# The mask gathers of the last four column pairs, moved from layer 0 to the first tiles of layer 1

## The chip, the cores and the metric

The kernel runs on one core of a Trainium2 chip. The metric is the time of one execution on the device in microseconds (us). A profile of one further execution goes with it: times inside the program come from that profile and count from the start of its span.

## The reference, cut to what matters

Four graph layers work on 4096 nodes with 256 features each. The graph is a 4096 x 4096 matrix `adj` of zeros and ones that is sparse and uneven: the first nodes have many neighbours, the late ones few. Every layer computes an attention over the neighbours, adds its input and normalizes.

```
# layer 0: eight heads, a bias from six curvature features
# layer 1: one head
H = X @ W_fc + b_fc
scores = (H @ w_att[:d])[:, None] + (H @ w_att[d:])[None, :] + b_att
alpha  = softmax(where(A > 0, scores, -1e9), axis=1)
x      = layernorm(x + alpha @ H)
# layer 2: four heads, elu, a residual and a second normalization
# layer 3: three attention layers in a row
```

In layer 1 the row's own score falls out of the softmax, so that a neighbour's weight depends on the neighbour alone, and the layer is a product of the mask (0 or 1) with prepared rows, divided by a sum.

## The kernel before, in words

**Pairs and lists.** Layers 1 to 3 work on `NP` = 16 "pairs" of `PW` = 256 output rows. A pair is either dense (all 32 tiles of 128 source nodes) or listed: layer 0 builds for it a list of those source nodes that have an edge into the pair, packed into `PAIR_TILES[q]` tiles of 128 nodes. The lists of pairs 1 to 15 have 251 tiles in all; the last four pairs, 12 to 15, have 14, 14, 13 and 13, together 54. In layer 1 the first six pairs are dense (`DENSE`), and the first `LEAD[1]` = 80 tiles that it works on are all dense; after them listed tiles and the remaining dense tiles alternate.

**What layer 0 prepares for the lists.** `list_pair(q)` computes two tables for each list: `pair_idx`, the node numbers, and `cell`, the place of each node's mask row in `adj` transposed. With it, `listed_mask` (L1000) makes one mask tile: POOL issues an indirect DMA that gathers 128 rows of 256 int32 from `adjT` into `pair_m` (L1003, 128 KB), DVE converts them to bytes in `pair_mb` (L1007), and SP writes these to `listed_d` in device memory (L1008). It returns the conversion as a function of its own, so that it can be run later. `job` starts one mask tile for each step of `lane` and runs a conversion when more than three are under way.

**Layer 0 itself.** `rows_by_edges` goes over blocks of up to ten tiles of edges. For each tile POOL gathers 128 rows from `table0` into `g` (L648). For each block DVE takes `d` from `g` (L655), PE and ACT make the pair terms (L657 to L667), DVE multiplies `g` by its weights (L679), and PE adds the rows up into `acc` (L692), beside products that place the edges (L628). Three buffers hold `g`, so the gathers of a block wait until L692 is done with the block three before it. Now and then `Ends0` finishes four chunks of rows: it normalizes them and projects them for layer 1 (L196 to L216). The mask tiles, the list building (L976, L982) and the rows of the one dense chunk (L498 to L525) run between the blocks.

**Layer 1.** `layer1` first prepares 32 tiles of rows: SP loads `V` (L1365), DVE and ACT scale it and split it into two pieces `Vp` (L1359, L1360, L1368), and POOL writes eight parts of `table` (L1370). Then `attend` runs through the sequence of tiles. For each tile `weights` turns a mask tile into `w` (L1382; ACT takes the tiles with odd count, DVE the others), for listed tiles gathers the node rows (L1284, POOL, 16 buffers) and splits them; `products` (L1393) multiplies two tiles behind. `ends_of` finishes a pair: sums, normalization, and the projection for layer 2. SP loads four mask tiles at once (L1278), into six buffers.

**What sets the order.** Each engine works off its own queue in order. Inside `attend`, the orders of PE, DVE and ACT are those of the program text (`manual_schedule`); elsewhere, and for POOL and SP, a scheduler places the instructions when the program is built. POOL has one queue for all gathers and for its table writes.

Of the kernel before, what the change touches and what calls it, by code (L numbers as in the profile page):

```python
# [52 lines left out]
U8 = mybir.dt.uint8  # L53
U16 = mybir.dt.uint16
I32 = mybir.dt.int32
# [6 lines left out]
P = 128  # L62
# [9 lines left out]
PW = 256  # L72
PAIR_TILES = [32, 25, 22, 20, 19, 18, 17, 16, 16, 15, 15, 14, 14, 14, 13, 13]
DENSE = {1: 6, 2: 1, 3: 3}
LEAD = {1: 80, 2: 32, 3: 44}


@with_exitstack
def gnn_stack(ctx: ExitStack, tc: tile.TileContext, a: dict, out: bass.AP):
# [19 lines left out]
    NP = N // PW  # L99
# [4 lines left out]
    keep = ctx.enter_context(tc.tile_pool(name="keep", bufs=1))  # L104
# [3 lines left out]
    def tags(pool, names):  # L108

        count = [0]  # L110

        def ps(shape, name):
            count[0] += 1
            return pool.tile(shape, F32, name=name, tag=names[count[0] % len(names)])
        return ps

    def drain(steps):
        for _ in steps:
            pass
# [201 lines left out]
    def row_tile(k):  # L321
        return epi.tile([P, C], F32, name=f"y{k % 4}", bufs=1)
# [271 lines left out]
    def rows_by_edges(prepared, pair_w, neg_bound, ends, ps, lane, first):  # L594
# [8 lines left out]
        with ExitStack() as st:  # L603
# [149 lines left out]
            ends.until(NC)  # L753
            drain(ends.steps)

    def layer0(proj):
        lin = 1.0 - 0.2
        with ExitStack() as st:
# [60 lines left out]
            lists = st.enter_context(tc.tile_pool(name="l0_list", bufs=2))  # L819
            pool = st.enter_context(tc.tile_pool(name="l0_ps", bufs=1, space=PSUM))  # L820
            ps = tags(pool, ["pa", "pb"])
            lists_ps = st.enter_context(tc.tile_pool(name="l0_list_ps", bufs=1, space=PSUM))

            jobs, dense_jobs = [], []
# [134 lines left out]
            def list_pair(q):  # L959


                A, Q, b = PAIR_TILES[q], NT // 4, q % BP
                at = ats[q // BP]
                cell = lists.tile([P, A], I32, name="cell", bufs=NP - 1)
                rhs = lists.tile([P, NT, 2, A], BF16, name="rhs", bufs=1)
                nc.vector.tensor_tensor(rhs[:, :, 1, :], count.unsqueeze(1)[:, :, 0:A].to_broadcast([P, NT, A]),
                                        at[:, 0, b, :].unsqueeze(2).to_broadcast([P, NT, A]), ALU.is_equal)
                yield
                nc.vector.tensor_tensor(rhs[:, :, 0, :], rhs[:, :, 1, :], tiles.unsqueeze(2).to_broadcast([P, NT, A]), ALU.mult)
                nc.vector.tensor_scalar_mul(rhs[:, :, 1, :], rhs[:, :, 1, :], row)  # L970
                yield
                pl = lists_ps.tile([P, 2, A], F32, name="list_p")

                def products(k, here):
                    for T in range(k * Q, (k + 1) * Q):
                        nc.tensor.matmul(pl, here[:, T - k * Q, :], rhs[:, T], start=T == 0, stop=T == NT - 1)  # L976

                due = []
                for k in range(4):
                    T = slice(k * Q, (k + 1) * Q)  # L980
                    here = lists.tile([P, Q, P], BF16, name="here", bufs=2)
                    nc.vector.tensor_tensor(here, count.unsqueeze(1).to_broadcast([P, Q, P]),  # L982
                                            at[:, 1, b, T].unsqueeze(2).to_broadcast([P, Q, P]), ALU.is_equal)
                    due.append((k, here))
                    yield
                    if len(due) > 1:
                        products(*due.pop(0))
                products(*due.pop(0))
                yield
                x = lists.tile([P, 2, A], F32, name="list")  # L990
                nc.vector.tensor_copy(x, pl)

                nc.vector.scalar_tensor_tensor(x[:, 0], x[:, 0], float(P), x[:, 1], ALU.mult, ALU.add)
                nc.vector.tensor_scalar_add(pair_idx[:, pair_at[q]:pair_at[q] + A], x[:, 0], float(N))
                nc.vector.tensor_scalar(x[:, 1], x[:, 0], float(N), float(N - 1), ALU.add, ALU.min)
                nc.vector.tensor_scalar(cell, x[:, 1], float(N // PW), float(q), ALU.mult, ALU.add)
                jobs.extend([lambda i=i: listed_mask(q, i, cell) for i in range(A)])
                yield

            def listed_mask(q, k, cell):  # L1000

                m = at_pool.tile([P, PW], I32, name="pair_m", bufs=5)
                nc.gpsimd.indirect_dma_start(m[:, :], None, pair_cells, bass.IndirectOffsetOnAxis(ap=cell[:, k:k + 1], axis=0))  # L1003

                def convert():
                    mb = at_pool.tile([P, PW], U8, name="pair_mb")
                    nc.vector.tensor_scalar(mb, m, 0.0, None, ALU.is_gt)  # L1007
                    nc.sync.dma_start(listed_d[:, pair_at[q] + k, :], mb)  # L1008
                return convert
# [150 lines left out]
            at_pool = st.enter_context(tc.tile_pool(name="l0_at", bufs=3))  # L1160

            for ic in range(-(-DENSE[1] * PW // IC)):
                dense_jobs.extend(mask_bytes(at_pool, ic))
            begun, dense_begun = [], []
            lanes = [[edge_lists, 0.0], [list_pairs(), 0.0]]
            ends = Ends0(proj, ps)
# [70 lines left out]
                given += 1  # L1237
        return order + rest[given:]

    def attend(seq, opened, weights, products, ends, rate=1.0, batch=1, lag=2):  # L1240

        states, ready, ended, due = {}, [], [], 0.0
        end = ends(ended)
        with tc.manual_schedule(engines={mybir.EngineType.PE, mybir.EngineType.DVE, mybir.EngineType.Activation}):
            def multiply(n):
                some, ready[:] = ready[:n], ready[n:]
                products(some)
                ended.extend(state for state, _, _, last in some if last)  # L1250

            for q, k, A, listed in seq:
                if k == 0:
                    states[q] = opened(q, A, listed)
                ready.append((states[q], k, weights(states[q], k), k == A - 1))
                if len(ready) == lag + batch:
                    multiply(batch)
                due += rate
                while due >= 1.0:
                    due -= 1.0  # L1260
                    next(end, None)
            while ready:
                multiply(min(batch, len(ready)))
            drain(end)

    class Nodes:
# [59 lines left out]
    def ends_of(ended, pairs, nxt, ps, one):  # L1326

        for _ in range(6):
            yield
        if nxt is not None:  # L1330
            yield from nxt.prepare(ps)
        for n in range(pairs):
            while not ended:
                yield
            yield from one(ended.pop(0), n)
# [7 lines left out]
    def layer1(proj, nxt, seq):  # L1343
        with ExitStack() as st:
            nxt.load(st)
            lp = st.enter_context(tc.tile_pool(name="l1", bufs=1))
            work = st.enter_context(tc.tile_pool(name="l1_work", bufs=6))
            got = st.enter_context(tc.tile_pool(name="l1_got", bufs=16))
            pool = st.enter_context(tc.tile_pool(name="l1_ps", bufs=1, space=PSUM))
            ps = tags(pool, ["pa", "pb"])  # L1350
# [38 lines left out]
            def products(some):  # L1389
                for (_, _, acc), k, (w, V), last in some:  # L1390
                    for it, t in enumerate(acc):
                        for i in range(2):
                            nc.tensor.matmul(t, w[:, it * P:(it + 1) * P], V[:, i, :], start=k == 0 and i == 0,  # L1393
                                             stop=last and i == 1)

            def one(state, n):
                q, _, acc = state
                xrs = [row_part(s1, q * PW + it * P) for it in range(RT)]
                yield
                ys = []  # L1400
                mv = epi.tile([P, RT, 2], F32, name="mv")
                for it, (t, xr) in enumerate(zip(acc, xrs)):
                    inv = inverse(t[:, C:C + 1].unsqueeze(1))
                    y = row_tile(n * RT + it)
                    nc.vector.scalar_tensor_tensor(xr, proj.cs, inv[:, 0:1], xr, ALU.mult, ALU.add)
                    nc.vector.scalar_tensor_tensor(y, t[:, 0:C], inv[:, 1:2], xr, ALU.mult, ALU.add)
                    moments(y, mv[:, it, :])
                    ys.append(y)
                    yield
                yield from norm_steps(ys, mv, s2, q * PW)  # L1410
                yield from project(nxt, ys, q * PW)

            attend(seq, opened, weights, products, lambda ended: ends_of(ended, NP, nxt, ps, one))
            nxt.sums()

    def residual(T, pr):
# [191 lines left out]
    def layers(p1, sparse):  # L1608

        def plan(n):  # L1610
            k = DENSE[n] if sparse else NP
            return sequence(range(k), range(k, NP), LEAD[n])

# [25 lines left out]
    with tc.If(nc.values_load(over[0:1, 0:1], min_val=0, max_val=1) > 0):  # L1639
        with ExitStack() as st:  # L1640
            pool = st.enter_context(tc.tile_pool(name="all_at", bufs=5))
            for ic in range(-(-DENSE[1] * PW // IC), NIC):
                for load in mask_bytes(pool, ic):
                    load()()
            p1 = first_projection()
            ps = tags(st.enter_context(tc.tile_pool(name="all_ps", bufs=1, space=PSUM)), ["pa", "pb"])
            p1.load(st)
            drain(p1.prepare(ps))
            pool = st.enter_context(tc.tile_pool(name="all_acc", bufs=2, space=PSUM))
            ends = Ends0(p1, ps)  # L1650
# [59 lines left out]
```

## Time and profile before

| | us |
|---|---|
| median of 3 runs | 3496.66 |
| runs, lowest to highest | 3496.36 to 3497.55 |
| the profiled execution's own time | 3482.08 |
| its span | 3480.4 |
| POOL busy | 1941.0 (56%) |
| PE busy | 2684.1 (77%) |
| DVE busy | 2300.2 (66%) |
| mean granted clock of PE | 0.824 |
| last mask gather of layer 0 starts | 1228.3 |
| last row gather of layer 0 starts | 1318.3 |
| first table write of layer 1 | 1380.9 |

POOL's busy time counts an indirect DMA only while POOL writes its descriptors; the landing of the data is later, and shows as the wait of whoever uses them. In lines of groups the columns are line, engine, operation, out<-in and count, then busy us and the mean ns of one, then the engine's idle time before them and what ended most of it. In timelines each line has the start, the duration, and in brackets the idle time before it. In lines of waits the numbers are us in total, times, and the longest. In lines of windows there are the busy us of the engines, with the number of instructions, then the clock, the share of the DMA engines and GB/s.

### The profile page before, as it was taken

To read this page: it belongs to the slowest core of one execution; us is meant where nothing else is said; L and a number is where in the kernel's file an instruction comes from. 1 tells how busy PE (TensorE), PEld (TensorE's weight loads), DVE (VectorE), ACT (ScalarE), POOL (GpSimd) and SP (SyncE) were. 2 spreads that over 40 slices of the span, in tenths; PEclk is the share of its full clock that TensorE was granted. 3 is DMA by queue.
4 is the path that set the end of the run, shared out by engine and by line. 5 is a ranking of instruction groups with operands and counts; after the bars stand their busy time and mean duration, and the time that the engine had idled before them with its cause. 6 is when DMAs were issued, how large, how long until landed. Compare 5 with 4: busy or idle time off the path is not lost. (4 is left out here: it accounts for less than half of the span.)

```text
span 3480.4 us, 53129 instructions
## 1 busy us (share of the span) xinstructions
PE 2684.1 (77%) x15814; PEld 1998.9 (57%) x15814; DVE 2300.2 (66%) x7414; ACT 1349.4 (39%) x3868; POOL 1941.0 (56%) x1874
## 2 busy tenths in 40 slices
PE   6475567767778766888688787777699989989885
PEld 5354455555556554777544333333488868867674
DVE  7798877786555443555488888778455545545665
ACT  3354446554445443455431222233312222232333
POOL 0264555666777761455158655553177637746772
PEclk8576656667787666988899999999799989989998
DMA  6587777664444443555343333332444454436552
GB/s 183 160 263 247 223 224 234 192 204 117 119 121 115 122 112 113 172 147 144 99 125 101 100 99 100 97 90 57 130 135 137 118 156 135 136 95 185 154 154 81
DMA packets 345903, 495.62 MB, mean 142 GB/s; under 512 B 120444, under 2 KB 252386, under 8 KB 345602
## 3 DMA queue, kind: packets, MB, share of 16 engines
q0 software_dynamic: 87600, 252.16, 25.9%
q1 hardware_dynamic: 239576, 223.18, 21.6%
q10 hardware_dynamic: 18432, 16.79, 1.4%
q8 instruction: 131, 2.15, 0.3%
q14 instruction: 164, 1.34, 0.1%
HBM read 426.20 MB, written 65.72 MB: 141 GB/s over the span
## 5 line engine op out<-in xcount | busy, mean ns | idle before, releaser
L1284 POOL DMA_INDIRECT g<-table,pair_idx x1010 | 1111.5, 1101 | 597.9 <-PE den L1487 95.8
L648 POOL DMA_INDIRECT g<-table,idx x445 | 502.1, 1128 | 285.2 <-issue 151.3
L1573 PE MATMUL acc<-g,w 128*128 128x257 f32 x2448 | 576.7, 384 | 36.3 <-DVE w L1567 36.3
L1573 PEld LDWEIGHTS acc<-g,w 128*128 128x128 f32 x2448 | 461.1, 191 | 112.6 <-DVE w L1567 49.0
L1474 DVE SCALAR_TENSOR_TENSOR w<-R,g,mask 128x256 f32<-128x256 f32 x1004 | 425.4, 493 | 23.0 <-PE den L1487 18.5
L1483 PE MATMUL num<-w,g 128*64 128x256 f32 x2008 | 319.5, 422 | 51.6 <-DVE w L1474 50.9
L1567 DVE SCALAR_TENSOR_TENSOR w<-R,g,mask 128x256 f32<-128x256 f32 x612 | 282.1, 480 | 100.4 <-PE acc L1573 98.0
L1003 POOL DMA_INDIRECT pair_m<-in_adjT,cell x251 | 269.7, 1075 | 136.7 <-issue 46.0
L692 PE MATMUL acc<-g,to_row 128*128 128x264 f32 x890 | 325.9, 528 | 18.3 <-DVE g L679 16.2
L1573 PE MATMUL acc<-V,w 128*128 128x257 f32 x1152 | 288.3, 390 | 22.4 <-DMA R<-r_d 17.5
L692 PEld LDWEIGHTS acc<-g,to_row 128*128 128x128 f32 x890 | 225.9, 268 | 77.6 <-DVE g L679 20.5
L1483 PEld LDWEIGHTS num<-w,g 128*64 128x64 f32 x2008 | 157.5, 148 | 196.1 <-DVE w L1474 135.0
L1573 PEld LDWEIGHTS acc<-V,w 128*128 128x128 f32 x1152 | 221.4, 195 | 60.2 <-ACT V L1553 18.1
L1583 ACT ACTIVATE y<-acc,inverse 128x256 f32<-128x256 f32 x96 | 45.6, 475 | 516.2 <-DVE inverse L318 444.2
L207 PE MATMUL ph<-wx,xT 128*128 128x258 f32 (+3 forms) x640 | 204.4, 456 | 34.7 <-ACT xT L198 30.0
L628 PE MATMUL x<-what,of_row 128*128 128x40 f32 (+4 forms) x890 | 157.1, 350 | 55.9 <-DVE of_row L625 54.3
L891 DVE FIND_INDEX8 cand<-ones,near 128x8 uint16<-128x520 bf16 (+8 forms) x424 | 195.0, 469 | 0.0
L628 PEld LDWEIGHTS x<-what,of_row 128*128 128x128 f32 x890 | 153.2, 265 | 66.4 <-DVE of_row L625 54.9
L686 ACT ACTIVATE to_row<-count,side 128x128 f32<-128x128 f32 x445 | 145.3, 391 | 115.1 <-PE acc L692 111.4
L1007 DVE TENSOR_SCALAR pair_mb<-pair_m 128x256 uint8<-128x256 int32 x251 | 74.8, 300 | 172.0 <-DMA pair_m<-in_adjT,cell 153.5
L1567 DVE SCALAR_TENSOR_TENSOR w<-R,V,mask 128x256 f32<-128x256 f32 x288 | 135.3, 480 | 69.9 <-PE acc L1573 55.1
L207 PEld LDWEIGHTS ph<-wx,xT 128*128 128x128 f32 x640 | 137.0, 224 | 73.9 <-ACT xT L198 44.8
(325 smaller groups left out, 4608.1 us busy)
## 6 DMA issues: line engine op xcount, KB each, us to landing
ai<-in_adj SPq DMA_DIRECT2D x124, 512.0 KB
mask<-listed_d SPq DMA_DIRECT2D x228, 128.0 KB
at<-in_adjT SPq DMA_DIRECT2D x96, 256.0 KB
mask<-mask_d SPq DMA_DIRECT2D x128, 128.0 KB
g<-table,pair_idx POOLq DMA_INDIRECT x1010
R<-r_d SPq DMA_DIRECT2D x56, 256.0 KB
table<-V POOLq DMA_DIRECT2D x12, 1032.0 KB
s<-y ACTq DMA_DIRECT2D x96, 128.0 KB
```

The source lines that it names most:

```text
L207: nc.tensor.matmul(ph, xT[:, kt, :], self.wx[:, kt, :], start=kt == 0, stop=kt == 1 and self.bias is None)
L628: nc.tensor.matmul(self.x[:, t], of_row[:, t], ls.what, start=True, stop=True)
L648: nc.gpsimd.indirect_dma_start(self.g[:, t, :], None, table0[:, :], bass.IndirectOffsetOnAxis(ap=self.idx[:, t:t + 1], axis=0))
L686: nc.scalar.activation(self.to_row[:, t], count, AF.Abs, bias=self.side[:, t, 0:1])
L692: nc.tensor.matmul(acc, self.to_row[:, t], self.g[:, t, 0:VW], start=self.t0 + t == 0, stop=last and t == n - 1)
L891: nc.vector.max_index(cand[:, s], ones8, near[:, at:at + W])
L1003: nc.gpsimd.indirect_dma_start(m[:, :], None, pair_cells, bass.IndirectOffsetOnAxis(ap=cell[:, k:k + 1], axis=0))
L1284: nc.gpsimd.indirect_dma_start(g[:, :], None, self.table[:, :], bass.IndirectOffsetOnAxis(ap=pair_idx[:, at:at + 1], axis=0))
L1474: nc.vector.scalar_tensor_tensor(w[:, h], R[:, h].rearrange("p t i -> p (t i)"), g[:, VW2 + h:VW2 + h + 1], m, ALU.max, ALU.mult)
L1483: nc.tensor.matmul(num[h % 2 * D2:(h % 2 + 1) * D2, h // 2, :], g[:, h * (D2 + 1):h * (D2 + 1) + D2], w[:, h], start=False, stop=last and ...
L1567: nc.vector.scalar_tensor_tensor(w, R[:, q * PW:(q + 1) * PW], g[:, C + 1:C + 2], m, ALU.max, ALU.mult)
L1573: nc.tensor.matmul(t, w[:, it * P:(it + 1) * P], g[:, 0:C + 1], start=k == 0, stop=last)
```

## The change

The gathers, conversions and writes of pairs 12 to 15 leave layer 0. `list_pair` still computes their `cell`, into lasting memory (`keep`), and puts the 54 steps into `late_jobs`. In layer 1, `attend` gets a further sequence of steps, `aside`, and takes one step of it for each tile, after that tile's weights and products. A step starts one mask gather, and converts the gather of three steps before. The tiles `pair_m` (five buffers) and `pair_mb` (three) of these steps lie in layer 1's pool `work`. Lines of the changed kernel stand some lines later: L1003 becomes L1010, L1007 L1014, L648 L650, L692 L694, L1382 L1391, L1284 L1293, L1370 L1379, L1393 L1402.

```diff
+LATE = 12
...
-                cell = lists.tile([P, A], I32, name="cell", bufs=NP - 1)
+                cell = lists.tile([P, A], I32, name="cell", bufs=LATE - 1) if q < LATE else keep.tile([P, A], I32, name=f"cell{q}")
...
-                jobs.extend([lambda i=i: listed_mask(q, i, cell) for i in range(A)])
+                if q < LATE:
+                    jobs.extend([lambda i=i: listed_mask(at_pool, q, i, cell) for i in range(A)])
+                else:
+                    late_jobs.extend([lambda pool, i=i: listed_mask(pool, q, i, cell) for i in range(A)])
...
-    def attend(seq, opened, weights, products, ends, rate=1.0, batch=1, lag=2):
+    def attend(seq, opened, weights, products, ends, rate=1.0, batch=1, lag=2, aside=iter(())):
...
                 if len(ready) == lag + batch:
                     multiply(batch)
+                next(aside, None)
...
+            drain(aside)
             drain(end)
...
+            def late_masks():
+
+                begun = []
+                while late_jobs:
+                    begun.append(late_jobs.pop(0)(work))
+                    if len(begun) > 3:
+                        begun.pop(0)()
+                    yield
+                for convert in begun:
+                    convert()
...
-            attend(seq, opened, weights, products, lambda ended: ends_of(ended, NP, nxt, ps, one))
+            attend(seq, opened, weights, products, lambda ended: ends_of(ended, NP, nxt, ps, one), aside=late_masks())
```

More of the change, by code (lines that the diff above doesn't have):

```diff
@@ L754, in rows_by_edges @@
             drain(ends.steps)
+    late_jobs = []
     def layer0(proj):
@@ L996, in list_pair, with listed_mask @@
                 nc.vector.tensor_scalar(cell, x[:, 1], float(N // PW), float(q), ALU.mult, ALU.add)
-                jobs.extend([lambda i=i: listed_mask(q, i, cell) for i in range(A)])
+                if q < LATE:
+                    jobs.extend([lambda i=i: listed_mask(at_pool, q, i, cell) for i in range(A)])
+                else:
+                    late_jobs.extend([lambda pool, i=i: listed_mask(pool, q, i, cell) for i in range(A)])
                 yield
-            def listed_mask(q, k, cell):
-                m = at_pool.tile([P, PW], I32, name="pair_m", bufs=5)
+            def listed_mask(pool, q, k, cell):
+                m = pool.tile([P, PW], I32, name="pair_m", bufs=5)
                 nc.gpsimd.indirect_dma_start(m[:, :], None, pair_cells, bass.IndirectOffsetOnAxis(ap=cell[:, k:k + 1], axis=0))
                 def convert():
-                    mb = at_pool.tile([P, PW], U8, name="pair_mb")
+                    mb = pool.tile([P, PW], U8, name="pair_mb", bufs=3)
                     nc.vector.tensor_scalar(mb, m, 0.0, None, ALU.is_gt)
```

## The prediction

> **What bounds the kernel now.** I read the page's groups first, for the price of one mask gather and of its conversion.
>
> ```profile
> L1284 POOL DMA_INDIRECT g<-table,pair_idx x1010 | 1111.5, 1101 | 597.9 <-PE den L1487 95.8
> L648 POOL DMA_INDIRECT g<-table,idx x445 | 502.1, 1128 | 285.2 <-issue 151.3
> ...
> L1003 POOL DMA_INDIRECT pair_m<-in_adjT,cell x251 | 269.7, 1075 | 136.7 <-issue 46.0
> ...
> L1007 DVE TENSOR_SCALAR pair_mb<-pair_m 128x256 uint8<-128x256 int32 x251 | 74.8, 300 | 172.0 <-DMA pair_m<-in_adjT,cell 153.5
> ```
>
> All gathers share POOL's one queue, and DVE lost 153.5 us waiting for mask gathers to land. Where that matters, POOL's own timeline shows, here near the end of layer 0:
>
> ```profile
> 1224.55 0.95 POOL L1003 DMA_INDIRECT pair_m<-in_adjT,cell  x1 [0.30 <-issue]
> 1225.80 0.95 POOL L1003 DMA_INDIRECT pair_m<-in_adjT,cell  x1 [0.30 <-issue]
> 1227.06 0.95 POOL L1003 DMA_INDIRECT pair_m<-in_adjT,cell  x1 [0.30 <-issue]
> 1228.31 0.95 POOL L1003 DMA_INDIRECT pair_m<-in_adjT,cell  x1 [0.30 <-issue]
> 1229.56 0.95 POOL L648 DMA_INDIRECT g<-table,idx  x1 [0.30 <-PE d_p L657]
> ```
>
> A gather costs POOL 0.95 + 0.30 = 1.25 us, back to back; a busy share of 76% is a full queue. The last 54 mask gathers lie between 1015.5 and 1228.3. The waits of 1015 to 1230 (three answers: DVE, PE, then POOL to 1320):
>
> ```profile
> DVE pair_mb L1007 <- DMA pair_m<-in_adjT,cell: 61.5, 21, 8.6
> DVE d L655 <- DMA g<-table,idx: 15.2, 3, 5.7
> ...
> PE d_p L657 <- DVE d L655: 25.3, 6, 9.5
> ...
> POOL g L648 <- PE acc L692: 24.4, 5, 15.1
> ```
>
> So in layer 0's tail POOL leads, but PE follows closely: POOL itself waits 24.4 us until acc (L692) has freed a row buffer. The windows say how closely (columns PE, PEld, DVE, ACT, POOL busy, clock, DMA):
>
> ```profile
> 1015.00:1060.00 45.00, 31.92 (x190) 24.89 (x191) 27.61 (x84) 24.47 (x71) 35.55 (x32) 0.77 0.48 130
> 1060.00:1100.00 40.00, 38.19 (x157) 27.66 (x156) 21.23 (x72) 21.07 (x70) 24.84 (x24) 0.67 0.36 101
> 1100.00:1150.00 50.00, 34.55 (x194) 27.64 (x193) 25.96 (x87) 22.64 (x56) 39.27 (x36) 0.70 0.47 125
> ```
>
> From 1015 to 1282 PE is busy 203 of 267 us. The other place is layer 1. POOL stands idle there, but only at certain times:
>
> ```profile
> 1380.86 0.82 POOL L1370 DMA_DIRECT2D table<-V  x1 [61.60 <-ACT w L1382]
> ...
> 1409.74 0.75 POOL L1370 DMA_DIRECT2D table<-V  x1 [4.51 <-DVE w L1382]
> 1414.31 1.01 POOL L1284 DMA_INDIRECT g<-table,pair_idx  x1 [3.82 <-issue]
> ...
> 1433.34 0.95 POOL L1284 DMA_INDIRECT g<-table,pair_idx  x1 [0.30 <-issue]
> 1451.54 0.94 POOL L1284 DMA_INDIRECT g<-table,pair_idx  x1 [17.26 <-DVE w L1382]
> ```
>
> Eight table writes end at 1410, 16 row gathers fill the 16 buffers by 1434, and POOL then waits 17 us for the first listed tile, tile 80. In the windows of L1393 (four matmuls to a tile) 131 matmuls are done by 1411 and 318 by 1451: tile 33 and tile 80, so 47 dense tiles in 40 us, 0.85 us each, with two pairs' ends among them.
>
> **What the skill says.** The Trainium skill, SBUF — State Buffer, section "SBUF: two separate sides": DVE and GpSimd share a port pair by an exclusive lock, and a GpSimd that writes DMA descriptors is held until the DVE operation ends. The trace agrees: the gather at 1216.44 took 2.81 us beside the 2.90 us L679 begun at 1215.53. I leave these stretches in both kernels. DMA: Bandwidth & Descriptors, "Anatomy of one DMA — SWDGE (gpsimd) path": about 2.0 us plus bytes/436e3, an estimate of 2.3 us for 128 KB; here a mask gather starting at 1224.55 let its conversion start at 1227.24, 2.7 us. I use the trace's. TensorE: Matmul & The Clock Gate, "What's actually happening": the clock is half unless activity releases it. The trace supports it only in part: 0.56 where PE was half idle (1200 to 1230), but 0.67 in 1060 to 1100 with PE busy 95%. I take no gain from the clock, and put it into the range.
>
> **The change, part by part.** POOL's order in the two programs is equal up to the last 54 mask gathers; then 155 row gathers of layer 0 follow without a mask, and the 54 stand in layer 1: 9 ahead of the first table write, 12 between the table writes and behind the last, the other 33 mixed with and behind the 16 row gathers. In layer 1 they are issued one per tile; the conversion comes three tiles later, in DVE's hand-written order, ahead of further w copies.
>
> (1) *Layer 0, POOL.* Removed: 54 x 1.254 = 67.7 us of queue. This is worth only what PE allows. In the mask-free 1230 to 1320, 55 row gathers take 90 us, 1.63 us each, at PE 79% busy. At that rate the 62 row gathers of 1100 to 1230 need 101 us of 130: 29 us won from 28 masks (35 us). Of 1015 to 1100, with 26 masks (33 us), PE is busy 70 of 85 us and still has the dense rows (L502, L525): at 90% it takes 78, about 8 us won; the six masks at 1075 to 1083 stand before a gather that waited for acc anyway. Behind 1230 the block delayed by the last four masks, which DVE awaits 9.5 us at 1246, catches up: 3 us. Sum **-40 us**. Bounds: at 84% PE (its share of 1000 to 1100) 203 us become 242, 25 won; with POOL alone the bound, 67.7 less the six useless ones and some slack, 58.
>
> (2) *Layer 0, DVE and SP.* 54 conversions of 0.30 us (16 us) and 54 writes of listed_d at 0.32 us leave. They ran within DVE's waits: inside (1), no extra.
>
> (3) *Layer 1, POOL.* The first 9 gathers (11 us) fit into the 61.6 us wait, as soon as layer 0's memory is free; there are five pair_m buffers, so the tenth waits for the fifth's conversion. Seven more (9 us) fit among the table writes, which wait on V anyway. From the last table write, 1410.5, POOL has 38 masks + 16 row gathers = 54 x 1.254 = 67.7 us, without a gap: until 1478. The last lands 2.7 us after its start, 1480, and its conversion stands ahead of tile 55's work. Before, tile 55 was reached at 1431. What waits: DVE for pair_m, behind it the odd tiles' w, behind those PE. Loss at tile 55: 49 us. The 25 tiles up to the first listed tile took 20 us and take 20 again: nothing gives the loss back, because POOL's 16 row gathers wait full in both kernels. With 1 us for a colder PE: **+50 us**. Bounds: 44 if V's preparation ends earlier, since fewer w copies stand in it; 57 if mask traffic slows V's loads and table writes.
>
> (4) *Layer 1, DVE and SP.* 54 x 0.30 us of conversion lie within DVE's new waits (it was busy 3 to 5 of 10 us): nothing. SP's 54 writes now stand between mask loads, and each waits for DVE; but these loads run some 20 tiles ahead (six buffers of four tiles): 0, at most 3 us. Of three pair_mb buffers one comes free after the landing of its write, faster than POOL delivers: 0. Without the POOL bound these would cost some 16 us of DVE time.
>
> (5) *cell* of four pairs in lasting memory: no instruction, 0.
>
> Sum -40 + 50 = +10 us. The profiled execution took 3482.08 us (span 3480.4), so 3492 for such a one; the runs' median is 3496.66, 14.6 above it, and +10 gives **3507 us**.
>
> **Rivals.** *Faster:* PE keeps up in layer 0, since its clock rises with activity; POOL stays the only bound and 58 us are won. For it: PE's L692 averages 497 ns in the mask-free stretch against 587 ns in 1100 to 1230. Against: POOL's 24.4 us of waits for acc. It decides once layer 0 wins more than 57 us: -58 + 46 = -12, 3485 us. *A draw:* 45 to 55 won, 50 lost: 3497. *Worse:* layer 0 wins only 25, because PE and the chain y, xT, ph of the row ends (a wait of 15 us at 1281 even without masks) take over, and layer 1 loses 55: +30, 3527. That the masks do not move is excluded by the order.
>
> **Numbers.** A run tells 0.2%, 7 us, from no change. Forecast (+7 to +21 us) 0.42, worse (+21 and over) 0.20, draw 0.22, faster 0.16. So slower 0.62, same 0.22, faster 0.16. The range takes the draw and most of the rivals: 3486 to 3527; the slower cases' own range is 3504 to 3527.
>
> **What would show it.** Right: no mask gather in layer 0 after about 1000 us; layer 0's last row gather (1318 before) at about 1278; then DVE waits of 1 to 2 us each for pair_m in layer 1, some 40 in a row, POOL back to back from the last table write for 68 us, PE half idle meanwhile, and L1284's seventeenth gather about 91 us behind the last table write, where it was 42. Wrong: a last row gather before 1260 (layer 0 wins more), or the seventeenth gather within 60 us of the last table write (the masks hide in layer 1).

## The result and the profile after

The changed kernel took 3506.95 us (median; 3501.39 to 3512.24), before it 3497.11 us in the same series. The ratio is 1.0027, with a 95% interval of 1.0009 to 1.0045: 10 us slower, between 3 and 16. Its profiled execution took 3501.39 us with a span of 3499.0 us, 18.6 us more than the span before. The groups, in the same columns as those shown of before:

```profile
L1293 POOL DMA_INDIRECT g<-table,pair_idx x1010 | 1126.9, 1116 | 592.5 <-issue 94.5 <-DVE w L1494 82.6 <-PE acc L1593 81.2
L650 POOL DMA_INDIRECT g<-table,idx x445 | 506.9, 1139 | 314.1 <-issue 136.5 <-PE acc L694 84.4 <-PE s L504 26.7
L1010 POOL DMA_INDIRECT pair_m<-in_adjT,cell x251 | 264.9, 1055 | 167.3 <-DVE pair_mb L1014 46.8 <-issue 42.3 <-DVE inverse L319 26.7
L1014 DVE TENSOR_SCALAR pair_mb<-pair_m 128x256 uint8<-128x256 int32 x251 | 74.9, 302 | 161.0 <-DMA pair_m<-in_adjT,cell 120.1 <-DMA listed_d<-pair_mb 22.6 <-issue 11.6
```

Only the reasons for waiting changed: POOL's waits for acc (L694) in layer 0 rose from 68.3 to 84.4 us, and mask gathers now wait for layer 0's memory too (26.7 us); their waits for conversions hardly changed (42.9 and 46.8 us). Counts and durations stay. The two places tell more. POOL's timeline, start and duration, then the idle time before:

```profile
1280.20 0.95 POOL L650 DMA_INDIRECT g<-table,idx  x1 [0.30 <-issue]
1281.45 0.94 POOL L650 DMA_INDIRECT g<-table,idx  x1 [0.30 <-issue]
1308.78 0.94 POOL L1010 DMA_INDIRECT pair_m<-in_adjT,cell  x1 [26.39 <-DVE inverse L319]
...
1345.50 0.82 POOL L1379 DMA_DIRECT2D table<-V  x1 [20.50 <-DVE V L1377]
...
1375.97 0.80 POOL L1379 DMA_DIRECT2D table<-V  x1 [3.18 <-DVE pair_mb L1014]
...
1444.13 0.95 POOL L1010 DMA_INDIRECT pair_m<-in_adjT,cell  x1 [0.30 <-DVE pair_mb L1014]
1472.18 0.94 POOL L1293 DMA_INDIRECT g<-table,pair_idx  x1 [27.11 <-DVE w L1391]
```

The last row gather of layer 0 starts at 1281.5 (1318.3 before). The last mask gather starts 68.2 us behind the last table write, and the seventeenth row gather 96.2 us behind it (41.8 before).

To compare traces whose starts differ, I cut each at five instructions: the 290th row gather of layer 0 (the next one opens the part without masks in the changed kernel), the last of its 445 row gathers, the first and the last table write of layer 1, and the seventeenth row gather of layer 1. The lengths in us, and the measured time against before with its interval:

| kernel | start of tail | tail of layer 0 | to first table write | to last | to 17th gather | time against before |
|---|---|---|---|---|---|---|
| before | 992.9 | 325.4 | 62.5 | 28.9 | 41.8 | 0 |
| changed | 1003.9 | 277.6 | 64.0 | 30.5 | 96.2 | +10 (3 to 16) |
| e_cells | 1009.0 | 325.4 | 61.1 | 28.9 | 40.5 | +1 (-4 to 5) |
| e_l0 | 1009.5 | 278.1 | 62.2 | 29.2 | 41.7 | -51 (-59 to -44) |
| e_l1 | 1003.1 | 325.5 | 62.8 | 30.9 | 95.2 | +56 (48 to 64) |
| e_still0 | 1010.3 | 320.6 | 62.8 | 29.9 | 42.9 | -2 (-7 to 2) |
| e_nowait | 1008.1 | 278.3 | 91.4 | 29.8 | 66.1 | +9 (5 to 14) |
| e_lag9 | 1007.3 | 277.8 | 63.4 | 31.3 | 92.3 | +5 (1 to 8) |
| e_half | 1010.8 | 275.7 | 63.2 | 29.7 | 64.8 | 0 (-4 to 4) |
| e_late14 | 1008.7 | 301.3 | 63.1 | 29.8 | 65.0 | +2 (-4 to 7) |
| e_v14 | 1005.5 | 278.0 | 65.9 | 35.8 | 45.5 | -26 (-33 to -19) |
| e_t20 | 1013.5 | 300.4 | 67.4 | 33.7 | 46.8 | -20 (-25 to -15) |
| e_best | 1010.6 | 278.2 | 66.9 | 35.1 | 63.2 | -25 (-31 to -18) |
| e_best2 | 1005.1 | 279.4 | 69.8 | 32.8 | 57.4 | -21 (-27 to -14) |

So in the changed kernel layer 0 gave 325.4 - 277.6 = 47.8 us, and layer 1, from its last row gather on, cost (64.0 + 30.5 + 96.2) - (62.5 + 28.9 + 41.8) = 57.5 us. The difference, +9.7 us, is the measured one. The remaining 9 of the 18.6 us between the two spans come from elsewhere: 11.0 us are lost ahead of the tail, and 2 us come back behind the seventeenth gather. On every engine the two traces have the same order of instructions until the first moved mask, so those 11 us are not of the change; the experiments confirm it.

Each row of the table is one execution, and its cuts don't always hold to the microsecond: those of e_v14, e_t20 and e_best add up to -33, -10 and -15 us, where the runs say -26, -20 and -25.

### The profile page after: what moved, and what is told of

Its sections match the earlier page's. It is cut to its first block, busy times and chain, and to the rows that moved or that the text cites. A ratio compares the mean times of both kernels' runs of the same rounds, so it can differ in the third digit from the quotient of the medians.

```text
span 3499.0 us, 53095 instructions
## 1 busy us (share of the span) xinstructions
PE 2682.3 (77%) x15814; PEld 2000.5 (57%) x15814; DVE 2303.5 (66%) x7414; ACT 1346.6 (38%) x3868; POOL 1956.6 (56%) x1874
## 5 line engine op out<-in xcount | busy, mean ns | idle before, releaser
L1293 POOL DMA_INDIRECT g<-table,pair_idx x1010 | 1126.9, 1116 | 592.5 <-issue 94.5
L650 POOL DMA_INDIRECT g<-table,idx x445 | 506.9, 1139 | 314.1 <-issue 136.5
L1010 POOL DMA_INDIRECT pair_m<-in_adjT,cell x251 | 264.9, 1055 | 167.3 <-DVE pair_mb L1014 46.8
L694 PE MATMUL acc<-g,to_row 128*128 128x264 f32 x890 | 317.1, 517 | 18.6 <-DVE g L681 17.9
L1593 PE MATMUL acc<-V,w 128*128 128x257 f32 x1152 | 289.2, 391 | 22.8 <-DMA R<-r_d 11.8
L694 PEld LDWEIGHTS acc<-g,to_row 128*128 128x128 f32 x890 | 221.0, 262 | 75.0 <-DVE g L681 22.7
L1603 ACT ACTIVATE y<-acc,inverse 128x256 f32<-128x256 f32 x96 | 45.5, 474 | 518.3 <-DVE inverse L320 446.1
L1402 PE MATMUL acc<-Vp,w 128*128 128x258 f32 x768 | 143.1, 328 | 55.7 <-DVE w L1391 51.6
```

The source lines that it names most:

```text
L650: nc.gpsimd.indirect_dma_start(self.g[:, t, :], None, table0[:, :], bass.IndirectOffsetOnAxis(ap=self.idx[:, t:t + 1], axis=0))
L694: nc.tensor.matmul(acc, self.to_row[:, t], self.g[:, t, 0:VW], start=self.t0 + t == 0, stop=last and t == n - 1)
L1293: nc.gpsimd.indirect_dma_start(g[:, :], None, self.table[:, :], bass.IndirectOffsetOnAxis(ap=pair_idx[:, at:at + 1], axis=0))
L1593: nc.tensor.matmul(t, w[:, it * P:(it + 1) * P], g[:, 0:C + 1], start=k == 0, stop=last)
```

## The experiments

### The two halves, and the 11 us ahead of both

e_cells moves only the `cell` tables:

```diff
-                cell = lists.tile([P, A], I32, name="cell", bufs=NP - 1)
+                cell = lists.tile([P, A], I32, name="cell", bufs=11) if q < 12 else keep.tile([P, A], I32, name=f"cell{q}")
```

> The kernel before with one edit: the cell tables of pairs 12 to 15 lie in lasting memory, as in the changed kernel; all 54 mask gathers stay in layer 0. The traces of before and after differ by 11 us at the start of the tail of layer 0, although no instruction is out of order there. Theory (step 5 of the prediction, placement costs nothing and the 11 us belong to that one execution): same time, within 3 us. Rival (the new place of the tables and of all that is placed behind them costs the 11 us): 8 to 11 us slower, and the 300th row gather of layer 0 starts about 10 us later than in the trace of before.

Measured: ratio 1.0002 (0.9988 to 1.0015), no difference. Its trace nevertheless starts the tail at 1009.0 us, 16 us behind the trace of before, and so does e_still0 (1010.3), where the tables lie as before. All thirteen other profiled executions start it between 1003.1 and 1013.5 us; the one of before, with 992.9, is the odd one: it took 3482.08 us, and none of the 19 runs of before in this series was below 3491. The rival, placement, falls: the later start that it names is in the trace, but it is there without the edit as well, and costs nothing in the times. On every engine e_cells has the order of before from the first instruction to the last, so these 16 us are a difference between two executions of the same order.

e_l0 gathers the 54 masks nowhere:

```diff
-            attend(..., aside=late_masks())
+            attend(...)
...
-... listed_d[:, at:at + n, :] if self.listed ...
+... listed_d[:, at - mask_shift(self.q):at - mask_shift(self.q) + n, :] if self.listed ...
...
+    def mask_shift(q):
+        return pair_at[q] - pair_at[q - 4] if q >= LATE else 0
```

> The layer-0 half alone: the 54 late mask tiles are gathered nowhere; in layer 1 to 3 pairs 12 to 15 load the mask tiles of pairs 8 to 11 instead (same number and size of loads, other values). Theory (the POOL queue leads and PE follows closely): 40 us faster (25 to 58), with the last row gather near 1278 us and POOL waiting for acc in the tail. If the 11 us ahead of the tail belong to the one execution of after, its own tail says 48 us faster. Rival (PE gets faster with its clock, POOL stays the only bound): 58 to 67 us faster, no waits of POOL for acc. Rival (row ends and PE take over): 25 us faster.

e_l1 leaves layer 0 whole and gathers the 54 again in layer 1:

```diff
-                if q < LATE:
-                    jobs.extend([lambda i=i: listed_mask(at_pool, q, i, cell) for i in range(A)])
-                else:
+                jobs.extend([lambda i=i: listed_mask(at_pool, q, i, cell, listed_d) for i in range(A)])
+                if q >= LATE:
+                    late_jobs.extend([lambda pool, i=i: listed_mask(pool, q, i, cell, again_d) for i in range(A)])
...
```

> The layer-1 half alone: layer 0 gathers all its masks as before, and layer 1 gathers the 54 a second time, one per tile, converts them and writes them to a scratch array that nothing reads. Theory (POOL's 54 gathers and 16 row gathers in one queue behind the last table write): 50 us slower (44 to 57), with the seventeenth row gather 91 to 96 us after the last table write. Rival (the gain and the loss are both smaller, and mask traffic of layer 0 hides in neither): under 40 us slower. With the layer-0 half the sum has to be the change's own +10 us; if it is not, the two halves act on one another.

Measured: e_l0 -51 us (ratio 0.9853, 0.9831 to 0.9874), e_l1 +56 us (1.016, 1.0138 to 1.0183). Their sum, +5, agrees with the change's +10 within the intervals, and the traces are closer still: the tail of e_l0 is within 0.5 us that of the changed kernel, and the 95.2 us of e_l1 are within 1 us its 96.2. The halves don't act on one another. Each is larger than predicted, and the rival "both are smaller" falls. In e_l0 POOL still waits for acc, 39.8 us in five times; so POOL did not stay the only bound there.

### Layer 0: POOL's queue, or DVE's waits?

In e_still0 all masks stay in layer 0, but the last 54 conversions wait for none:

```diff
-                    nc.vector.tensor_scalar(mb, m, 0.0, None, ALU.is_gt)
+                    nc.vector.tensor_scalar(mb, m if q < 12 else still[0], 0.0, None, ALU.is_gt)
...
```

> The kernel before with the waits of the last 54 conversions of layer 0 taken away: they convert a tile that is filled beforehand (listed_d gets no real masks for pairs 12 to 15), while all 54 gathers stay in POOL's queue in layer 0. It tells which part of the 48 us that layer 0 gives up is POOL's queue, and which is DVE's waiting in order for the gathers (61.5 us in 1015 to 1230). Theory (POOL's queue is what costs): 0 to 10 us faster than before. Rival (DVE's waits cost, POOL's queue has room): 35 to 48 us faster.

Measured: 0.9993 (0.998 to 1.0006), and a tail of 320.6 us, 4.8 shorter. The waits of 1015 to 1250 in e_still0 tell why:

```profile
DVE d L655 <- DMA g<-table,idx: 73.8, 10, 15.3
PE d_p L657 <- DVE d L655: 46.8, 8, 10.9
```

DVE's 61.5 us of waiting for mask gathers are gone, and in their place it waits 73.8 us for row gathers, 15.2 before. A wait at the end of a full queue only changes its name. So DVE's waits are not what the 54 masks cost in layer 0, and POOL's queue is what is left: 67.7 us less of it make 47.8 us. Two smaller parts leave layer 0 together with it and were not taken away alone: the conversions' own 16 us of DVE time, and the writes.

### Layer 1: what the 57 us consist of

e_nowait takes the conversions' wait away in layer 1:

```diff
-                    nc.vector.tensor_scalar(mb, m, 0.0, None, ALU.is_gt)
+                    nc.vector.tensor_scalar(mb, m if still is None else still, 0.0, None, ALU.is_gt)
...
```

> The changed kernel with the wait of the 54 conversions taken away: they stand where they stood in DVE's order, but convert a tile that is filled beforehand, so that listed_d gets no real masks for pairs 12 to 15. All 54 gathers still go through POOL's queue. Theory (the loss of 57 us has two parts, tiles held up because DVE waits in order for each gather, and row gathers queued among the masks): the dense tiles run at their old pace, and the seventeenth row gather waits only for POOL's queue, which is busy until 68 us after the last table write; before, it came 42 us after. So about 27 us of loss stay and 30 go: 18 to 25 us faster than before the change. Rival (POOL's queue alone sets the loss): as slow as the changed kernel, 5 to 12 us slower than before. Rival (all of it is DVE's wait): 40 to 48 us faster.

Measured: 1.0027 (1.0015 to 1.004), like the changed kernel. But this run doesn't answer its question. Since no conversion held the buffers any more, POOL issued 51 of the 54 gathers ahead of the first table write, which came 28.9 us later behind the last row gather of layer 0 than before the change; the loss only moved. Something else showed. The three `pair_mb` buffers became a limit: behind 1395 us conversions waited 17.8 us for the landing of their writes. And the tiles stood still while `V` was prepared, although no conversion waited for a gather. With three masks behind the last table write, the seventeenth row gather still came 24.3 us later behind it than before the change. The changed kernel has the same halt. The windows count the matmuls of the tiles, four to a tile (columns PE and PEld busy, with the counts, then clock and DMA). The first line of each kernel is the 31 us up to its last table write. Before:

```profile
1378.74:1409.74 31.00, 22.61 (x123) 20.00 (x124) 0.80 0.77 235
1409.74:1431.94 22.20, 13.97 (x101) 12.48 (x100) 0.92 0.57 169
1431.94:1452.74 20.80, 14.17 (x106) 12.99 (x105) 1.00 0.33 100
```

After:

```profile
1344.97:1375.97 31.00, 10.60 (x58) 9.52 (x57) 0.72 0.86 244
1375.97:1448.37 72.40, 36.66 (x160) 31.58 (x160) 0.62 0.57 156
1448.37:1473.47 25.10, 17.56 (x105) 16.23 (x106) 0.77 0.23 71
```

In the preparation 31 tiles became 15. DVE's and ACT's orders in the traces show the reason: before, 35 of their copies to `w` stand ahead of the last piece of `Vp`, after it 16. The conversions stand in DVE's hand-written order between these copies, and the scheduler, which mixes the preparation into that order, put the pieces of `Vp` ahead. In the changed kernel this need not cost anything: the second line is POOL's time, 72.4 us until tile 55 (which came 22.2 us behind the last table write before), and tile 57 could not come before the last mask in any case. The third line is dearer than before: 26 tiles in 25.1 us instead of 20.8, with a clock of 0.77 instead of 1.00; nearly the same number of instructions (125 and 126, the ends of pairs among them) kept PE busy 22.8 us instead of 17.7.

e_lag9 has eleven `pair_m` buffers and converts nine tiles after the gather:

```diff
-                m = pool.tile([P, PW], I32, name="pair_m", bufs=5)
+                m = pool.tile([P, PW], I32, name="pair_m", bufs=5 if q < LATE else 11)
...
-                    if len(begun) > 3:
+                    if len(begun) > 9:
```

> The changed kernel with eleven pair_m buffers in place of five, and each conversion nine tiles after its gather in place of three. Theory (the loss is counted from where POOL's queue stands at the last table write): six more gathers run ahead of the first table write, 7.5 us; the last conversion stands at tile 63 in place of 57, about 5 us of tiles at full pace; so the loss falls from 57 to about 45 us: 0 to 6 us faster than before the change. Rival (DVE's waits come from a lag too short for the 2.7 us landing, not from POOL's rate): most of the loss goes, 25 us faster or more. Rival (POOL's order fills up with row gathers instead): no change against the changed kernel.

Measured: 1.0013 (1.0004 to 1.0022), some 5 us better than the changed kernel (the two intervals overlap), and 3.6 us in the trace; 12 were expected. Only 11 gathers, not 15, came ahead of the first table write (9 in the changed kernel): with the longer lag no conversion freed a buffer in that time. The last mask gather came 64.1 us behind the last table write instead of 68.2. And the last conversion did not move to tile 63: once the 54th gather is started, `late_masks` runs all conversions that are left in one step, so in both traces the last one stands behind 27 of DVE's copies to `w`, and the 5 us expected of it could not come. The rival, a lag too short for the landing, needed 25 us and falls: nearly all conversions stood later and little was won, so the landing is not the bound.

e_half starts one mask for every second tile:

```diff
+            def sparse(steps, n):
+                for _ in steps:
+                    for _ in range(n):
+                        yield
...
-            attend(..., aside=late_masks())
+            attend(..., aside=sparse(late_masks(), 2))
```

> The changed kernel with one late mask for every second tile in place of every tile. Theory (what costs in layer 1 is tiles that wait in order for POOL's gathers, 1.25 us each against 0.85 us for a tile): at half the rate POOL keeps up with the dense tiles, except for the 16 row gathers that join its queue at the last table write (16 x 1.25 = 20 us, of which some 10 are slack), and some 14 masks fall among the listed tiles, where POOL is nearly full (another 14 us). So the loss falls from 57 to about 24 us: 20 to 28 us faster than before the change. Rival (the loss is POOL's total work, wherever it stands behind the table): no change against the changed kernel, 5 to 12 us slower than before.

Measured: 1.0 (0.9989 to 1.0012), so 10 us better than the changed kernel (the two intervals just overlap), but not the 30 expected. The seventeenth row gather comes 64.8 us behind the last table write, 23 more than before, and up to the last listed row of layer 1 another 23 us are lost (250.1 us instead of 226.8; 225 to 234 in the other traces), where the remaining masks meet the listed tiles' gathers. The first loss had been put at 10: the sixteen row gathers stand ahead of masks that are due, POOL works without a gap for 50 us from the last table write on, and the tiles wait for it. The rival was nearer: most of the loss is POOL's total work behind the table. But neither theory has the size, and the rate is not the only thing that changed: with conversions in every second tile alone, 23 tiles were done at the last table write, not 15.

e_late14 moves only 26 masks (`LATE = 14`).

> The changed kernel with LATE = 14: only the 26 mask tiles of pairs 14 and 15 move. In the trace of before these lie at 1133 to 1228 us. Theory: layer 0 gains 24 to 30 us (they stand in the stretch where POOL leads most). In layer 1 some 16 of 26 are issued by the last table write, 10 follow, 12.5 us and 2.7 us for the last landing, and tile 29 would have been due at the last table write: 12 to 18 us of loss. In sum 8 to 16 us faster than before. Rival (gain and loss are proportional to the number of masks, as they are for 54: 26/54 of +10): 2 to 7 us slower.

Measured: 1.0005 (0.999 to 1.002), between 4 us faster and 7 slower: the theory falls, and the rival's 2 to 7 us are not excluded. Layer 0 gives 24.1 us, the lower end of what was expected. Layer 1 costs 24.7 instead of 12 to 18. Ten masks follow the last table write as foreseen, but with four row gathers among them, and the last starts 17.4 us behind it, not 12.5. And the estimate took tile 29 as due at the last table write; again only 15 tiles were done by then, so that tile 30 came 24.5 us behind it. The last mask lands some 20 us behind it (17.4 and 2.7), so I read the rest as the cost of the halt that the changed kernel hides behind POOL.

### Other places for the same 54 masks

e_v14 starts them while `V` is prepared, outside the sequence of tiles:

```diff
+            late = late_masks()
+            for _ in range(14):
+                next(late, None)
             _, fs = extremes(lp, ps, proj.f2, 1)
...
                 nc.gpsimd.dma_start(table[...], V)
+                for _ in range(5):
+                    next(late, None)
+            drain(late)
...
```

> The changed kernel with the 54 late masks at another place: 14 steps ahead of the preparation of layer 1, 5 steps behind each of its eight table writes, eleven pair_m buffers in place of five, none in the sequence of tiles. Theory (the loss in layer 1 comes from putting the gathers behind the last table write, while POOL stood idle before it): layer 0's gain stays and layer 1 loses 0 to 15 us, so 25 to 40 us faster than before. Rival (the conversions hold up the preparation of V in DVE's queue, so that the table writes come as much later as POOL is busier): layer 1 loses 30 to 50 us, so between 10 us faster and 10 us slower than before.

Measured: 0.9925 (0.9905 to 0.9945), 26 us faster than before. Its POOL timeline:

```profile
1349.35 0.82 POOL L1393 DMA_DIRECT2D table<-V  x1
...
1385.14 0.81 POOL L1393 DMA_DIRECT2D table<-V  x1
...
1395.27 0.95 POOL L1010 DMA_INDIRECT pair_m<-in_adjT,cell  x1 [0.31 <-DVE rs L337]
...
1430.67 0.94 POOL L1293 DMA_INDIRECT g<-table,pair_idx  x1 [16.87 <-DVE w L1408]
```

32 gathers now run ahead of the first table write, in the time in which POOL had stood idle, and POOL waits again 16.9 us ahead of the seventeenth row gather, as before the change (17.3). Layer 0's gain stays (278.0), and layer 1 loses 14.0 us: 3.4 to the first table write, 6.9 between the writes, 3.7 behind.

e_t20 was to start 20 of them even earlier, behind the last row gather of layer 0:

```diff
+            for n in range(20):
+                begun.append(late_jobs.pop(0)(at_pool))
+                if len(begun) > 3:
+                    begun.pop(0)()
...
```

> The 54 late masks at a third set of places: 20 at the end of layer 0 behind its last row gather (in layer 0's own five buffers), 14 ahead of layer 1's preparation, the rest three behind each table write, none in the sequence of tiles. The version with 14 and 5 lost 14 us in layer 1, because POOL was still busy at the last table write (it came 102 us after the last row gather, before the change 91). Theory (POOL's queue at the table writes is what is left of the loss): with 25 us of gathers started earlier the table writes come 91 to 95 us after the last row gather, layer 1 loses 0 to 6 us, and the kernel is 40 to 48 us faster than before. Rival (masks at the end of layer 0 hold its memory longer, and layer 1's preparation starts later for it): first table write 10 or more us later than in the version with 14 and 5; 10 to 25 us faster than before.

Measured: 0.9942 (0.9928 to 0.9957). The edit didn't do what it says: the scheduler put these 20 among the row gathers of the tail, which grew to 300.4 us again. Neither theory was tested. It shows only that 20 masks back in the tail cost 22.8 us there, 1.1 us each, nearly POOL's 1.25.

e_best and e_best2 put most of them ahead of the preparation and the rest, thinly, into the tiles (e_best: 22, two behind each table write, 16 one for every third tile; e_best2: 26, one, 20):

```diff
-            for _ in range(14):
+            for _ in range(22):
...
-                for _ in range(5):
+                for _ in range(2):
...
-            drain(late)
...
-            attend(...)
+            attend(..., aside=sparse(late, 3))
```

> The 54 late masks at a fourth set of places, with eleven buffers: 22 ahead of layer 1's preparation, two behind each of the eight table writes, the other 16 one for every third tile. Theory (POOL's idle time before the table is complete holds 54 gathers, and only those queued ahead of a table write or ahead of a tile that is due cost anything): the loss of 14 us of the version with 14 and 5 shrinks to 2 to 8 us: 38 to 46 us faster than before. Rival (conversions among the preparation in DVE's queue set that loss, not POOL's order): 20 to 30 us faster, like the version with 14 and 5.

> As the version with 22 and 2, but 26 ahead of layer 1's preparation, one behind each table write and the other 20 one for every third tile. Theory: the same as there, with the table writes a little later at the start and less disturbed after it: 36 to 46 us faster than before. Rival: 20 to 30 us faster.

Measured: 0.993 (0.9912 to 0.9948) and 0.9941 (0.9924 to 0.9959): the rival's size for both. In e_best's trace the gain sought was lost behind the last table write (63.2 us to the seventeenth row gather, 45.5 in e_v14). The same windows of the tiles' matmuls in e_best, up to its last table write and behind it:

```profile
1359.76:1390.76 31.00, 0.00 (x0) 0.00 (x0) 0.50 0.90 251
1390.76:1412.96 22.20, 19.68 (x144) 19.02 (x144) 0.90 0.67 191
```

Not one tile in 31 us: with conversions in the tiles' hand-written order again, nearly all pieces of `Vp` went ahead of the tiles (5 of the copies to `w` started before the last piece). In e_best2 it was 7 tiles by the last table write. e_v14, which has more of them among the preparation but none there, keeps the order of before (31 tiles done at the last table write). So the rival has the size right but hardly the reason, and I read the result as the cost of that order; a version with POOL's places of e_best and the tile order of e_v14 was not run.

## Why the prediction was right, and where it was off

**The sum** was +10 us, and +9.7 came of it, but both terms were 8 us too small and their errors cancelled. The trade as such was foreseen, and the two halves run alone confirm it; that the sum was this close is luck.

**Step 1, layer 0: -40 predicted, -47.8 measured.** Cut at the same row gathers, the stretch of 1100 to 1230 fell from 128.5 to 101.7 us, where 101 was predicted. Behind it 2.6 us were won (predicted 3), and 1.2 ahead of 1022. The term that failed is "at 90% it takes 78, about 8 us won" (85 less 78 is 7): from 1022 to 1102 the same gathers took 63.4 us instead of 80.6, so 17.2. The windows, before and after (PE, PEld, DVE, ACT, POOL busy, clock, DMA):

```profile
1021.70:1102.30 80.60, 66.55 (x320) 50.17 (x320) 46.01 (x148) 42.52 (x127) 57.22 (x50) 0.72 0.42 116
1102.30:1230.80 128.50, 90.02 (x417) 69.12 (x415) 63.27 (x183) 49.92 (x132) 99.46 (x89) 0.66 0.44 118
```

```profile
1031.50:1094.80 63.30, 53.19 (x351) 42.03 (x348) 38.71 (x120) 42.19 (x131) 35.47 (x28) 0.85 0.32 89
1094.80:1196.60 101.80, 78.34 (x403) 60.76 (x402) 56.14 (x154) 50.44 (x134) 70.58 (x63) 0.75 0.38 104
```

PE's share of the first stretch is the same (83% and 84%), and lower than the 90% allowed. What the prediction had wrong is PE's own time: it held 70 us for fixed and took "no gain from the clock". PE needed 53 us where it had needed 67, with more matmuls in the stretch than before (351 and 320); 53 us at 84% make the 63. In these two traces the clock rose from 0.72 to 0.85, and L692 took 433 ns instead of 522.

It would be easy to book the difference to the clock, but the other traces don't allow that. Here is the same stretch, between the same two row gathers, in e_cells, which has all its masks in layer 0, and in e_best2, which has none of the 54 there:

```profile
1039.20:1117.40 78.20, 61.26 (x343) 47.19 (x342) 46.30 (x148) 42.48 (x128) 57.20 (x51) 0.80 0.43 117
1032.10:1097.10 65.00, 57.54 (x336) 45.26 (x336) 39.35 (x120) 39.83 (x124) 35.98 (x29) 0.76 0.31 85
```

The first has the higher clock and is the longer. In the four traces with 22 masks in this stretch it takes 78.2 to 80.6 us at clocks of 0.72 to 0.80; in the eight with none, 62.0 to 65.3 us at 0.76 to 0.86. So its length goes with the masks in POOL's queue. Why PE's time shrinks with it (61 to 67 us with masks, 53 to 58 without) stays open: the clock may be one part and the mix of PE's work, which differs between the orders, another, and no run separates them. The Trainium skill, TensorE: Matmul & The Clock Gate, section "What's actually happening", says that activity releases the throttle; over stretches of this length PE's busy share doesn't tell the clock (0.72 at 83% and 0.85 at 84%, 0.80 at 78% in e_cells and 0.76 at 89% in e_best2).

The rival "faster" was right that PE would keep up better than the forecast had it; its reason, the clock, is not shown. It needed 57 us. That POOL did not stay the only bound shows in its waits for acc, which between 1000 and 1290 us were longer than the 24.4 us of before:

```profile
POOL g L650 <- PE acc L694: 37.1, 6, 12.7
```

**Step 2** holds for the waits: e_still0 shows that the conversions' waiting in layer 0 costs no more than 5 us of its own. What the 54 conversions themselves cost there was not tried apart.

**Step 3, layer 1: +50 predicted, +57.5 measured.** The loss at tile 55 is 72.4 - 22.2 = 50.2 us, 49 predicted, and the last mask gather came 68.2 us behind the last table write, where POOL's queue was predicted to last 67.7. Two small terms were mis-sized. Tiles 55 to 80 cost 4.3 us more than before, where "1 us for a colder PE" was allowed (clock 0.77 instead of 1.00, and 5.1 us more of PE's time for nearly the same number of instructions). And the table writes came 3.1 us later, of which the prediction had only the upper bound, mask traffic. The lower bound, "44 if V's preparation ends earlier, since fewer w copies stand in it", saw that copies would leave the preparation, but drew the wrong sign from it: it ended no earlier, and the tiles were pushed behind it. DVE's waits for `pair_m` came, but not as some 40 of 1 to 2 us each; from 1376 to 1447 us they are (us in total, times, longest):

```profile
DVE pair_mb L1014 <- DMA pair_m<-in_adjT,cell: 33.5, 18, 5.2
```

**Steps 4 and 5.** The cells cost nothing (e_cells). Step 4's "0" for the three `pair_mb` buffers is not quite so: in the changed kernel, too, DVE waited for the landing of a write four times in layer 1, 7.2 us in all, 4.9 of them ahead of the first table write. In e_nowait, where the conversions followed faster, it was 17.8 us behind 1395 us alone.

**The base.** To forecast against the profiled execution and then add the 14.6 us to the median was right: that execution of before was 10 to 20 us ahead of all others by the tail of layer 0, and its lead says nothing of the kernel. Read against it, the change's +9.7 us looks like 18.6.

## What to carry to other kernels

A gather moved off a full queue is worth at most its time in that queue (here 47.8 us for 67.7, since the next engine follows closely), and costs about that time wherever the next engine waits in order behind it; look for the stretch in which the queue is idle and nothing due stands behind, here the wait ahead of the first table write (26 us faster instead of 10 slower). Work that is put into a hand-written order also changes what the scheduler puts around it: count the instructions ahead of a landmark in both kernels before pricing the wait. And cut two traces at common instructions before comparing spans, since a lead from earlier stages is otherwise booked to the change.

## What the runs showed of the hardware

The granted clock differed most: over the same 28 row gathers of layer 0 it was 0.72, 0.85, 0.80 and 0.76 in before, the changed kernel, e_cells and e_best2, with PE busy 83, 84, 78 and 89%. Behind the stretch in which the changed kernel's tiles waited for masks (PE busy 58%, clock 0.62) it was 0.77, where before the change it was 1.00. It also differs between executions of the same order: in the first 40 us a run of 64 small products (`cw_p`, L1054) took 251 ns each (median) in the trace of before and 356 ns in that of e_cells, and 356 in that of the changed kernel, which was 4.3 us behind by their end.

The landing of a conversion's 32 KB write, which its buffer waits for, held DVE up to 2.2 us in e_nowait, and once 4.9 us in the changed kernel. And the gather that the prediction saw held up beside a DVE product (L679) is no single case: in the trace of before, 47 gathers start while an L679 runs, and each ends 0.8 us or more behind its end. The prediction states it for any DVE operation; the section of the Trainium skill that it names (SBUF — State Buffer, "SBUF: two separate sides") limits it to some kinds of operation, and here it is shown for L679 alone.
